# A sort moved from behind a gather pass to behind the first experts, its transposes split over single PSUM banks, and one comparison reading its numbers from PSUM

## The chip, the cores and the metric

One Trainium2 chip, one of its cores. The time is the device time of one execution in microseconds (us), the median of three runs. The engines are named as in the profile: PE is the matrix engine (PEld its weight loads), DVE the vector engine, ACT the scalar engine, POOL the engine that issues the indirect DMAs, SP the queue for most plain DMAs. [...]

## The reference

A graph network of two layers on 6250 nodes with 256 features each, all in float32. Cut to the order of the work:

```python
edge_index = jnp.stack([src, dst])            # 100000 edges, 6250 nodes
xn = layernorm(x)
x = x + hconv2(xn, edges, edge_weight) + mix0(xn)      # layer 0: two convolutions, each
                                                       # h = relu(x @ w1 + b1)
                                                       # agg = segment_sum(ew * h[src], dst)
                                                       # h = relu(bn(agg @ w2 + b2))
x = x + ffn0(layernorm(x))                    # 8 experts, top 2 by a softmax gate
xn = layernorm(x)
x = x + gnn1(xn, edges, edge_attr) + mix1(xn) # gnn1: z_in[in_deg] + z_out[out_deg]
                                              #   + two sigmoid terms
                                              #   + segment_sum(edge_attr @ W_sum + b_sum, src)
x = x + ffn1(layernorm(x), edge_index2)       # 131072 edges of its own: attention over them
                                              # gives the gates of 4 experts
```

The list that this change moves is `edge_index2`, the edge list of the last layer: it has to be sorted by destination before the attention can run over it.

## The kernel before

The nodes lie in 49 tiles of 128. The node features `xa` stay on chip the whole time; `BT` holds a transposed working copy.

**Stages, in order of time.** (1) `first`: layer norm, transposes and the first dense product of every tile; the product goes to a DRAM table. (2) The first edge pass, in `aggregate(1, 0.75)`. (3) `convolve` and the second table. (4) The second edge pass, in `aggregate(2, 0.65)`. (5) `convolve`, then `gating`, which ends with the gates of the first experts. (6) `middle`: the eight first experts, with the edge sums of the second layer beside them. (7) `between` and `gat`: the second mixing, the attention over the sorted list, the four last experts.

**An edge pass** (`edge_pass`) takes 782 groups of 128 edges. For a group, POOL gathers 128 rows into one of 15 ring buffers (L751), DVE writes a 128x128 one-hot matrix by comparing `self.numbers`, which is 0 to 127 in PSUM, with the node of every edge (L591, L593 in `mark`), and PE multiplies rows by one-hot into the PSUM tile `es`, four groups to one tile (L578). DVE adds each finished tile into `BT` (L569). `es` has two banks. In the first pass ACT scales the rows by the edge weights (L615) and one more product counts degrees (L586). A row has 1024 bytes in the first two passes and 512 in the third, which runs in stage (6) and has one product to a group in place of two.

**The order around these passes is written out by hand.** Inside `manual_schedule`, each turn of the edge loop, or each step of the experts, calls `self.step(us)`. This runs the generator that was given to `after_this` until it has issued work worth `us`; what a piece is worth is the number that the piece yields. These numbers are estimates in the code and not measured times. `beside(work, other, rate)` weaves two generators: for every unit that `work` yields, `other` is given `rate` units. At the end `finish()` issues what is left.

In `experts` there are 808 steps: for every expert and every quad of tiles four steps with a first product (L1149, then Gelu on ACT, L1151) and for every tile one step with a second product (L1157) and two additions on DVE (L1161). The one tag `mm` of PSUM tiles serves both products; in stage (6) it has four buffers.

**The sort** (`bitonic`) holds 131072 keys as a 128x1024 tile and runs 153 stages of compare and exchange, each two DVE instructions of 128x512 (L216 and L217), or four of 128x256 (L224), from one tile `sx` to another, `sy`, or back. Where the exchange distance runs over partitions, `across` transposes the tile in eight pieces on PE (L230) into the PSUM tile `back`, which has two banks and one buffer, and ACT copies it back (L232); that happens 14 times in a sort. The kernel sorts twice: `sort_src` behind the first edge pass, after `mix0`, and `sort_gat` (`edge_index2`) behind the second, after `out_degrees`.

`out_degrees` counts how many edges leave each node: one DVE instruction makes eight one-hot matrices (L1175, 98 times), PE sums them over the partitions (L1181), and DVE adds the row to `deg` (L1186).

In stage (6) the generator beside the edge sums is `others()`: `gat_places` finds where each node's run begins in the sorted list (49 small counts, L701, then 49 gathers of 512 KB and counts of 1024 elements, L715), and `node_terms` makes the sigmoid and degree terms of the second layer (L1228 to L1242) and writes them to DRAM (L1243).

[...] `psum(mm, es)` shares them out: up to stage (4) `mm` 2, `es` 2, `kv` 1, `numbers` 1 and `back` 2; in stages (5) and (6) `mm` 4, `es` 2 and `numbers` 1, the stage having no `kv`.

Of the kernel before, what the change touches and what calls it, by code (L numbers as in the profile page):

```python
# [8 lines left out]
F32 = mybir.dt.float32  # L9
# [8 lines left out]
P = 128  # L18
# [33 lines left out]
class Net:  # L52
# [17 lines left out]

    def tr(self):
        return self.mm()

    def back(self):
        return self.ps.tile([P, 2, 512], F32, tag="back", name="back", bufs=1)

    def bcast(self, src, n):

# [123 lines left out]
    def bitonic(self, x, y, out):  # L202
# [4 lines left out]
        nc = self.nc  # L207
        cur, nxt = x, y
# [16 lines left out]
                                                   op0=OP.mult, op1=op)  # L225

        def across(src, dst):
            ps = self.back()
            for j in range(8):
                nc.tensor.transpose(ps[:, j // 4, j % 4 * P:(j % 4 + 1) * P], src[:, j * P:(j + 1) * P], self.ident)  # L230
            for i in range(2):
                nc.scalar.copy(dst[:, i * 512:(i + 1) * 512], ps[:, i, :])  # L232

        a, b = halves(cur, 2)
        nc.vector.tensor_scalar(b, b, -1.0, None, op0=OP.mult)
        yield 0.6
        for k in range(1, 18):
            if k > 10:
                across(cur, nxt)
                cur, nxt = nxt, cur  # L240
                yield 4.0
                for q in range(k - 11, -1, -1):
                    src = cur
                    if q < k - 11:
                        plain(src, nxt, 1 << q)
                    elif k < 17:
                        turned(src, nxt, 1 << q)
                    else:
# [5 lines left out]
                across(cur, nxt)  # L254
                cur, nxt = nxt, cur
                yield 4.0
            for d in range(min(k, 10) - 1, -1, -1):
                src = cur
                if k == 1 or k > 10 or d < k - 1:
                    plain(src, nxt, 1 << d)  # L260
                elif k < 10:
                    turned(src, nxt, 1 << d)
                else:

                    (a, b), (lo, hi) = halves(src, 1 << d), halves(nxt, 1 << d)
                    nc.vector.tensor_scalar(a, a, self.turn[:, 0:1], None, op0=OP.mult)
                    nc.vector.scalar_tensor_tensor(lo, b, self.turn[:, 1:2], a, op0=OP.mult, op1=OP.min)
                    nc.vector.scalar_tensor_tensor(hi, b, self.turn[:, 1:2], a, op0=OP.mult, op1=OP.max)
                cur, nxt = nxt, cur
                yield 1.3  # L270
# [259 lines left out]
    def sort_gat(self, pool):  # L530


        nc = self.nc
# [4 lines left out]
        xi, yi = x.bitcast(I32), y.bitcast(I32)  # L538
        nc.sync.dma_start(xi, ei[1].rearrange("(p w) -> p w", p=P))
        nc.sync.dma_start(yi, ei[0].rearrange("(p w) -> p w", p=P))  # L540
        yield 1.0
        nc.vector.tensor_scalar(xi, xi, NP - 1, None, op0=OP.min)
        nc.vector.tensor_scalar(xi, xi, NODE_BITS, NODE_ONE, op0=OP.logical_shift_left, op1=OP.bitwise_or)
        yield 2.0
# [137 lines left out]
    def gat_places(self, sp):  # L682
# [8 lines left out]
        nc.vector.tensor_scalar(li, li, NODE_BITS, NODE_ONE, op0=OP.logical_shift_left, op1=OP.bitwise_or)  # L691
        heads = sp.tile([P, 1], F32, name="heads")
        nc.sync.dma_start(heads.bitcast(I32), self.by_gat[:, 0:1])
        ph = self.tr()
        nc.tensor.transpose(ph[:, 0:P], heads.to_broadcast([P, P]), self.ident)
        hrow = sp.tile([P, P], F32, name="hrow")
        nc.vector.tensor_copy(hrow, ph[:, 0:P])  # L697
        runs = sp.tile([P, NT], F32, name="gruns")
# [187 lines left out]
    def aggregate(self, layer, us):  # L886
# [3 lines left out]
        with self.tc.tile_pool(name="degree", bufs=1) as dp:  # L890
# [4 lines left out]
            with self.tc.tile_pool(name="edges", bufs=1) as ep, self.tc.tile_pool(name="behind", bufs=1) as bp:  # L895
                if layer == 1:
                    self.after_this(self.mix0(bp), self.sort_src(bp))
                else:
                    self.after_this(self.out_degrees(bp, deg), self.sort_gat(bp))
                with self.tc.manual_schedule():  # L900
                    for _ in self.edge_pass(ep, self.BT, mine, self.table, self.src_of, self.node_of, self.w_of,
                                            self.base1, us):
# [266 lines left out]
    def out_degrees(self, pool, deg):  # L1169

        nc = self.nc
        for k0 in range(0, W1C, 8):
            n = min(8, W1C - k0)
            hot = pool.tile([P, 8, P], BF16, name="ohot", bufs=2)
            nc.vector.tensor_tensor(hot[:, 0:n, :], self.iota.unsqueeze(1).to_broadcast([P, n, P]),  # L1175
                                    self.from_of[:, k0:k0 + n].unsqueeze(2).to_broadcast([P, n, P]), op=OP.is_equal)
            yield 1.1
            ps = self.mm()
# [68 lines left out]
    def middle(self, scales, sums):  # L1247
# [4 lines left out]
        with self.tc.tile_pool(name="experts", bufs=1) as ep:  # L1252
# [2 lines left out]
            self.norms1 = self.norms(sums, "mix1")  # L1255
            with self.tc.tile_pool(name="edge", bufs=1, reuse_waits="tile") as edge:
                def others():
                    yield from self.alone(self.gat_places)
                    yield from self.alone(self.node_terms)
                self.after_this(self.beside(self.edge_sums(edge), others(), 0.45))  # L1260
                with self.tc.tile_pool(name="ffn0", bufs=1, reuse_waits="tile") as pool:
                    self.experts(pool, self.BT, g, 1.7)
        self.edge_pass_if(self.wide2, self.sumsT, None, self.a["edge_attr_128"], self.by_src,
                          EDGE_BITS, E1 - 1, None)

# [525 lines left out]
    def run(self):  # L1791
# [3 lines left out]
        self.load_x()  # L1795
        with tc.tile_pool(name="keep", bufs=1, side="right") as keep, ExitStack() as until:
            self.BT = keep.tile([P, 2, NP], F32, name="BT")
            with self.psum(2, 2) as self.ps:
                self.count_up()
                lists = until.enter_context(tc.tile_pool(name="lists", bufs=1, side="right"))  # L1800
                self.edge_of = lists.tile([P, NG * GE], I32, name="edge_of")
# [45 lines left out]
```

## Time and profile before

| | us |
|---|---|
| median of three runs | 6544.78 (6537.61 to 6550.44) |
| the profiled execution, its own time | 6529.97 |
| its span, first to last instruction | 6528.2 |
| second edge pass, first to last gather | 1607.9 to 2790.8 |
| first experts with the third edge pass | 2959 to 4544 |
| busy: PE, PEld, DVE, ACT, POOL | 4489.9, 3254.1, 3020.2, 1195.9, 3459.5 |

The profile is of one execution. A group of instructions is named by line, engine and operation, with output and inputs; behind it stand the busy time, the mean duration in ns and the idle time of the engine just before, with what ended it. The windows view gives the busy time of each engine in a stretch of time, with the number of instructions in brackets, the clock granted to PE (1 is full speed) and the share of time that the DMA engines were busy. "remote" and "another core or an unknown queue" name a releaser that the profile doesn't identify. A product in float32 shows as two PE instructions.

### The profile page before, as it was taken

The numbers are of one execution on the slowest core, as the hardware profiler recorded it, in microseconds if no ns is written. First come the engines' busy times: TensorE is split into PE (matmuls) and PEld (weight loads), VectorE is DVE, ScalarE is ACT, GpSimd is POOL, SyncE is SP. The second block draws the span as 40 slices with busy tenths as digits, with TensorE's granted clock in tenths as the row PEclk, the third lists the DMA queues.
The fourth block names the chain that finished last, engine by engine and source line by source line (L and its number), as shares of the span: only waits on it lengthen the run. The fifth ranks groups of instructions, "written<-read, shape, count | busy, mean of one in ns | idle before, by whom it ended". The sixth has DMA issues, their size and how long they took to land. (4 is left out here: it accounts for less than half of the span.)

```text
span 6528.2 us, 60427 instructions
## 1 busy us (share of the span) xinstructions
PE 4489.9 (69%) x19240; PEld 3254.1 (50%) x19240; DVE 3020.2 (46%) x8077; ACT 1195.9 (18%) x2327; POOL 3459.5 (53%) x3404
## 2 busy tenths in 40 slices
PE   3788687786656555479989999999932654555560
PEld 2566565554554445456667677676810332333340
DVE  5666465526676556265544555556500111111136
ACT  1333233334000000052111222212300111111120
POOL 0566477751777777604546556564257345554402
PEclk9767756668886766668999999999965777777685
DMA  4433322231332233321341222211221111111134
GB/s 152 126 102 100 99 85 85 86 93 52 89 87 84 85 88 90 91 65 54 118 85 50 63 65 65 64 49 47 71 57 16 38 33 34 33 40 33 34 106 148
DMA packets 356303, 483.23 MB, mean 74 GB/s; under 512 B 114311, under 2 KB 268598, under 8 KB 355926
## 3 DMA queue, kind: packets, MB, share of 16 engines
q0 software_dynamic: 140688, 305.56, 17.7%
q1 hardware_dynamic: 181308, 150.91, 7.8%
q10 hardware_dynamic: 33948, 22.47, 1.1%
q8 instruction: 164, 2.69, 0.2%
q14 instruction: 195, 1.60, 0.1%
HBM read 393.78 MB, written 85.31 MB: 73 GB/s over the span
## 5 line engine op out<-in xcount | busy, mean ns | idle before, releaser
L751 POOL DMA_INDIRECT ring<-table,src_of x1564 | 1701.4, 1088 | 1086.9 <-issue 313.2
L578 PE MATMUL es<-hot,ring 128*128 128x128 f32 x7820 | 1702.8, 352 | 542.6 <-DVE BT L569 192.0
L578 PEld LDWEIGHTS es<-hot,ring 128*128 128x128 f32 x7820 | 1393.7, 242 | 884.0 <-issue 406.3
L751 POOL DMA_INDIRECT G<-gtab,glist x800 | 766.0, 957 | 678.2 <-DVE msg L1572 401.7
L751 POOL DMA_INDIRECT ring<-in_edge_attr,edge_of x782 | 747.2, 955 | 686.5 <-PE es L578 291.5
L1764 PE MATMUL mm<-lw,lhT 128*128 128x256 f32 x1568 | 441.8, 411 | 611.0 <-ACT lhT L1758 336.1
L1157 PE MATMUL mm<-mw,hT 128*128 128x256 f32 x3136 | 747.5, 381 | 23.8 <-DVE xa L1161 20.4
L1149 PE MATMUL mm<-BT,mw 128*128 128x512 f32 (+1 forms) x1664 | 748.6, 573 | 10.0 <-DVE hrow L697 6.3
L1764 PEld LDWEIGHTS mm<-lw,lhT 128*128 128x128 f32 x1568 | 318.2, 205 | 795.5 <-issue 406.0
L1766 DVE TENSOR_TENSOR ly<-mm,lb 128x256 f32<-128x256 f32 x196 | 81.0, 422 | 1324.4 <-remote 553.3
L1157 PEld LDWEIGHTS mm<-mw,hT 128*128 128x128 f32 x3136 | 573.4, 192 | 115.8 <-DVE xa L1161 23.5
L1756 PE MATMUL mm<-lxt,lw 128*128 128x512 f32 (+1 forms) x832 | 425.1, 628 | 118.3 <-issue 116.2
L1151 ACT ACTIVATE hT<-mm,mb 128x512 f32<-128x512 f32 (+1 forms) x416 | 273.0, 661 | 1078.8 <-PE mm L1149 664.9
L1161 DVE SCALAR_TENSOR_TENSOR xa<-mm,gates,xa 128x256 f32<-128x256 f32 x392 | 189.1, 482 | 589.5 <-PE mm L1157 280.7
L615 ACT ACTIVATE ring<-ring,w_of 128x256 f32<-128x256 f32 x782 | 368.2, 502 | 491.1 <-DMA ring<-table,src_of 432.3
L569 DVE TENSOR_TENSOR BT<-BT,es 128x256 f32 x392 | 162.4, 414 | 501.1 <-remote 259.2
L1149 PEld LDWEIGHTS mm<-BT,mw 128*128 128x128 f32 x1664 | 287.0, 193 | 202.9 <-issue 188.2
L1758 ACT ACTIVATE lhT<-mm,lb 128x512 f32<-128x512 f32 (+1 forms) x208 | 135.9, 663 | 1315.9 <-remote 655.7
L593 DVE TENSOR_SCALAR hot<-numbers,node_of,w_of 128x128 f32<-128x128 f32 x782 | 291.2, 402 | 142.2 <-remote 67.3
L591 DVE TENSOR_SCALAR hot<-numbers,node_of 128x128 f32<-128x128 f32 x782 | 247.3, 338 | 165.7 <-PE es L578 101.9
L1756 PEld LDWEIGHTS mm<-lxt,lw 128*128 128x128 f32 x832 | 169.7, 210 | 254.1 <-issue 241.0
L591 DVE TENSOR_SCALAR hot<-numbers,from_of 128x128 f32<-128x128 f32 x782 | 249.9, 343 | 0.0
(854 smaller groups left out, 4315.9 us busy)
## 6 DMA issues: line engine op xcount, KB each, us to landing
ring<-table,src_of POOLq DMA_INDIRECT x1564
ye<-ly SPq DMA_DIRECT2D x48, 512.0 KB
yes<-ye SPq DMA_DIRECT2D x48, 512.0 KB
G<-gtab,glist POOLq DMA_INDIRECT x800
table<-h SPq DMA_DIRECT2D x98, 128.0 KB
ring<-in_edge_attr,edge_of POOLq DMA_INDIRECT x782
grows<-gs SPq DMA_DIRECT2D x10, 960.0 KB
mw<-in_L_ffn_W SPq DMA_DIRECT2D x16, 512.0 KB
```

The lines of the kernel that those rows point to most:

```text
L569: nc.vector.tensor_tensor(dst, dst, ps[:, 0:h * P].rearrange("p (j n) -> p j n", j=h), op=OP.add)
L578: nc.tensor.matmul(ps[:, j * P:(j + 1) * P], lhsT=rows[:, j * P:(j + 1) * P], rhs=hot, start=(first and j == 0), stop=(last and j == h - 1))
L591: self.nc.vector.tensor_scalar(dst, self.numbers, node, None, op0=OP.is_equal)
L593: self.nc.vector.tensor_scalar(dst, self.numbers, node, w, op0=OP.is_equal, op1=OP.mult)
L615: nc.scalar.activation(r, r, AF.Copy, scale=w[:, i:i + 1])
L751: self.nc.gpsimd.indirect_dma_start(out=dst, out_offset=None, in_=table, in_offset=bass.IndirectOffsetOnAxis(ap=idx, axis=0))
L1149: nc.tensor.matmul(ph[:, :n * P], lhsT=w1[:, j, c * P:(c + 1) * P], rhs=xT[:, j, t * P:(t + n) * P], start=(j == 0), stop=(j == 1))
L1151: nc.scalar.activation(hT[:, c, :n * P], ph[:, :n * P], AF.Gelu, bias=b1[:, e, c:c + 1])
L1157: nc.tensor.matmul(po[:, :C], lhsT=h0[:, i, c * P:(c + 1) * P], rhs=w0[:, i, :], start=(i == 0), stop=(i == 3))
L1161: nc.vector.scalar_tensor_tensor(x, y, g[:, t0 + c, e0:e0 + 1], x, op0=OP.mult, op1=OP.add)
L1756: nc.tensor.matmul(ph[:, :n * P], lhsT=w1[:, e, j, c * P:(c + 1) * P], rhs=xt[:, j, :n * P], start=(j == 0), stop=(j == 1))
L1764: nc.tensor.matmul(po[:, :C], lhsT=h0[:, i, c * P:(c + 1) * P], rhs=w2[:, e0, i, :], start=(i == 0), stop=(i == 3))
```

## The change

`sort_gat` is no longer given to the second edge pass. It becomes the first part of `others()` in stage (6), in its own pool, ahead of `gat_places`. The rates of that stage are set anew: `beside` gets 0.85 in place of 0.45, and a step of the experts is worth 2.2 in place of 1.7.

`across` no longer has a tile of two banks of its own. It takes two ordinary `mm` tiles of one bank each, and it yields in three places (4.0, 2.0, 2.0) where it was issued in one piece and its caller yielded 4.0 after it. Both sorts use it. The two banks set free go to `mm`: four in place of two up to the end of stage (4). In stages (5) and (6) `mm` gets five in place of four.

`out_degrees` compares with `self.numbers` in PSUM where it compared with `self.iota` in SBUF. `gat_places` yields 12.0 between loading the heads of the list and transposing them, and 3.0 before copying the transpose out.

```diff
         def across(src, dst):
-            ps = self.back()
+            yield 4.0
+            ps = [self.mm(), self.mm()]
             for j in range(8):
-                nc.tensor.transpose(ps[:, j // 4, j % 4 * P:(j % 4 + 1) * P], src[:, j * P:(j + 1) * P], self.ident)
+                nc.tensor.transpose(ps[j // 4][:, j % 4 * P:(j % 4 + 1) * P], src[:, j * P:(j + 1) * P], self.ident)
+            yield 2.0
             for i in range(2):
-                nc.scalar.copy(dst[:, i * 512:(i + 1) * 512], ps[:, i, :])
+                nc.scalar.copy(dst[:, i * 512:(i + 1) * 512], ps[i])
+            yield 2.0
...
-                across(cur, nxt)
+                yield from across(cur, nxt)
                 cur, nxt = nxt, cur
-                yield 4.0
...
         nc.sync.dma_start(xi, ei[1].rearrange("(p w) -> p w", p=P))
         nc.sync.dma_start(yi, ei[0].rearrange("(p w) -> p w", p=P))
-        yield 1.0
+        yield 10.0
...
         nc.sync.dma_start(heads.bitcast(I32), self.by_gat[:, 0:1])
+        yield 12.0
         ph = self.tr()
         nc.tensor.transpose(ph[:, 0:P], heads.to_broadcast([P, P]), self.ident)
+        yield 3.0
...
-                    self.after_this(self.out_degrees(bp, deg), self.sort_gat(bp))
+                    self.after_this(self.out_degrees(bp, deg))
...
-            nc.vector.tensor_tensor(hot[:, 0:n, :], self.iota.unsqueeze(1).to_broadcast([P, n, P]),
+            nc.vector.tensor_tensor(hot[:, 0:n, :], self.numbers.unsqueeze(1).to_broadcast([P, n, P]),
...
                 def others():
+                    yield from self.alone(self.sort_gat)
                     yield from self.alone(self.gat_places)
                     yield from self.alone(self.node_terms)
-                self.after_this(self.beside(self.edge_sums(edge), others(), 0.45))
+                self.after_this(self.beside(self.edge_sums(edge), others(), 0.85))
...
-                    self.experts(pool, self.BT, g, 1.7)
+                    self.experts(pool, self.BT, g, 2.2)
...
-            with self.psum(2, 2) as self.ps:
+            with self.psum(4, 2) as self.ps:
...
-                with self.psum(4, 2) as self.ps:
+                with self.psum(5, 2) as self.ps:
```

More of the change, by code (lines that the diff above doesn't have):

```diff
@@ L72, in tr @@
         return self.mm()
-    def back(self):
-        return self.ps.tile([P, 2, 512], F32, tag="back", name="back", bufs=1)
     def bcast(self, src, n):
@@ L253, in bitonic @@
                     yield 1.3
-                across(cur, nxt)
+                yield from across(cur, nxt)
                 cur, nxt = nxt, cur
-                yield 4.0
             for d in range(min(k, 10) - 1, -1, -1):
```

## The prediction, made before the changed kernel ran

> **What bounds the kernel now.** The change touches two stages, so I read the windows view by stage first. The second edge pass is cut where its companion work changes: beside `out_degrees` (1606 to 1984), beside the sort (1984 to 2598), alone (2598 to 2790). The first table holds the ring's instructions alone, the POOL column being the gathers.
>
> ```profile
> 1606.00:1984.00 378.00, 166.81 (x996) 143.80 (x996) 0.00 (x0) 290.55 (x251) 0.85 0.31 88
> 1984.00:2598.00 614.00, 326.84 (x1592) 280.04 (x1592) 0.00 (x0) 451.73 (x397) 0.68 0.30 85
> 2598.00:2790.00 192.00, 96.62 (x515) 87.69 (x514) 0.00 (x0) 126.40 (x134) 0.68 0.32 94
> ```
>
> Per gather that is 378/251 = 1.506 us, 614/397 = 1.547 us and 192/134 = 1.433 us; POOL is busy for 1.157, 1.138 and 0.943 us of each. So a gather is 0.2 us longer beside the companions, yet the pass alone is only 0.11 us a gather faster: something else stops it. The timeline shows both, first beside the sort, then alone.
>
> ```profile
> 2069.57 0.68 DVE L216 TENSOR_TENSOR sy<-sx 128x512 f32<-128x512 f32 x1
> 2070.17 0.69 DVE L217 TENSOR_TENSOR sy<-sx 128x512 f32<-128x512 f32 x1
> 2070.25 1.43 POOL L751 DMA_INDIRECT ring<-table,src_of  x1 [0.30 <-issue]
> 2070.77 0.73 DVE L593 TENSOR_SCALAR hot<-numbers,node_of,w_of 128x128 f32<-128x128 f32 x2
> ...
> 2710.54 0.95 POOL L751 DMA_INDIRECT ring<-table,src_of  x1 [0.30 <-issue]
> 2713.68 0.42 DVE L569 TENSOR_TENSOR BT<-BT,es 128x256 f32 x1 [13.63 <-remote]
> 2714.16 3.78 PE L578 MATMUL es<-hot,ring 128*128 128x128 f32 x16 [10.19 <-issue]
> 2718.19 0.94 POOL L751 DMA_INDIRECT ring<-table,src_of  x1 [3.33 <-PE es L578]
> ```
>
> A gather that meets the sort's two SBUF operands takes 1.43 us and more; alone it takes 0.95 with 0.30 to the next, a floor of 1.25. Then DVE stands 13.63 us for an unnamed releaser, PE with it, the ring fills and POOL waits 3.33 us.
>
> The first experts, in the table with all engines:
>
> ```profile
> 3510.00:4310.00 800.00, 796.46 (x3296) 559.85 (x3295) 459.06 (x1244) 175.81 (x316) 471.51 (x488) 1.00 0.22 63
> 4310.00:4522.00 212.00, 211.28 (x923) 151.41 (x922) 118.21 (x366) 36.15 (x56) 135.88 (x143) 1.00 0.17 45
> ```
>
> PE is busy for 99.6% at full clock. This stage is bound by PE, and all added to PE is paid in full. A step there, from the timeline:
>
> ```profile
> 3906.16 1.88 PE L1149 MATMUL mm<-BT,mw 128*128 128x512 f32 x4
> 3907.88 0.38 PE L578 MATMUL es<-hot,ring 128*128 128x128 f32 x2
> 3908.10 1.89 PE L1157 MATMUL mm<-mw,hT 128*128 128x256 f32 x8
> ```
>
> From start to start a step is 1.72 us and an edge group 0.22. 808 x 1.72 + 782 x 0.22 = 1562 us; the stage took 1585 (2959 to 4544). The rest is two waits: 6.3 us for `hrow` at the start, 20.1 us where DVE waits 30.1 us for `gend` in `gat_places`.
>
> [...] 1.43 us beside L216/L217, 0.95 beside L569 (SBUF and PSUM) and L593. [...] The page counts 164 and 195 packets on two instruction queues, and stalls of 10 to 14 us recur on PE and DVE; that these are fetches isn't shown.
>
> **The change, part by part.** I sum against the profiled execution, 6529.97 us, which is 15 us under the median of 6544.78; the same difference is then taken from the median.
>
> *Second pass, sort gone.* Removed: 153 compare stages on DVE, 112 transposes, 28 ACT copies, three DMAs on SP. 397 gathers go from 1.547 to the 1.433 of the stretch alone: **-45 us**. Bounds: the unaccompanied end of the first pass (1308 to 1446, 94 gathers) ran at 1.468, giving -31; the floor of 1.25 gives -118. I take 1.433, as the stalls stay.
>
> *Second pass, numbers in PSUM.* L1175 (98 x 1.203 us) now has one SBUF input, so it should no longer hold up gathers: 251 x (1.157 - 0.943) = 54 us of POOL. But beside it PE has 7.1 instructions a gather (1770/251) against 3.8, and DVE is busy for 265 of 378 us, so other stalls take over. I take 1.47 in place of 1.506: **-9 us**. Bounds: 1.433 gives -18[...].
>
> *First pass, `across` in three pieces.* Before, ACT stood behind transposes just issued: at 954 it had waited 14.8 us and then ran 12 row scalings in one burst. `sort_src` becomes 14 x 4 = 56 units longer: (259.7 of `mix0` + 316.5)/0.75 = 768 turns of 793, so it still ends inside the pass. The pass beside the sort runs at 493/318 = 1.55 us a gather, POOL's own 375.9/318 + 0.30 = 1.48; at most 22 us are there. **-10 us** (0 to -22).
>
> *Two more `mm` banks in stages 1 to 4.* PE waited for DVE to free a bank 15.6 us at L851 and 10.4 us at L158, mostly hidden. **-4 us** (0 to -12).
>
> *First experts, PE.* 14 x 8 = 112 transposes; sixteen took 3.41 us at full clock (4553.81), 0.21 each: **+24 us**, no cover. The `hrow` wait goes, since 12 units now lie between load and transpose: **-6 us**. The `gend` wait stays.
>
> *First experts, pacing.* Units: `sort_gat` 325.5, `gat_places` 122.3, `node_terms` 254.5, together 702; edges 793 x 1.27 = 1007. 1709 of 808 x 2.2 = 1778, so all ends by step 777, and nothing is left for `finish`. While both run, a step carries 2.2/1.85 = 1.19 units of edges (0.94 groups; before 1.7/1.45 = 1.17) and 1.01 of others (before 0.53). After step 695 a step carries 1.73 groups, PE needs 2.1 us and POOL 1.73 x 1.25 = 2.16; **+3 us** (0 to 8).
>
> *First experts, DVE.* Without others DVE's share is (459 - 154 us of `node_terms` groups)/412 steps = 0.74 us a step. A compare stage takes 1.20 us from start to start (1.43 for L224) and 1.01/1.3 = 0.78 of one falls to a step: 0.95. 1.69 of 1.93 us, 88%. In `gat_places` 1.35 us per 1.68 steps make 80%. In `node_terms` 3.14 us per 4.5 steps make 75%; before L1228 DVE waited 42 us in 49 tiles for the `terms` write, with half the distance now maybe 2 us each, which makes 98%. Behind DVE's waits stand the additions L1161, which free `mm`; five banks are five steps, some 9 us of slack. So short lags are hidden, lasting ones not: **+15 us** (0 to +60).
>
> *Queues.* SP gets two loads and a store of 512 KB each; behind them stand the next expert's weights, wanted over 100 us later, and the ten units (some 19 us) cover the loads. POOL has only the longer gathers: at 1.8 us against 1.93 x 1.06 = 2.05 a group it holds. Where `gat_places` reuses the sort's memory, its iota and the DVE instruction after it wait for the list's store, about 5 us, within the slack: **+2 us** (0 to 5).
>
> Sum: -45 - 9 - 10 - 4 + 24 - 6 + 3 + 15 + 2 = **-30 us**: 6500 for a profiled execution, **6515** as a median.
>
> **Rivals.**
> 1. *The second pass keeps its pace.* Stalls, not gathers, set it, and the sort's stretch comes only to 1.49 (-23), `out_degrees` and the first pass give nothing: -23 - 4 + 38 = +11, about 6556. For it: a 0.2 us longer gather showed as only 0.11. Against: the stretch alone is in the trace. Its lesser form is that the PSUM operand frees nothing, 9 us.
> 2. *DVE becomes the bound of the first experts* (slower). It decides from 1.93 us a step, 0.24 more than I count. Counted by durations (0.68 each) the compare stages come to 0.74 + 1.06 = 1.80, and L224 and PE waits may bring 2.1: 322 steps x 0.17 = 55, and `node_terms` 252 x 0.07 = 18. +73 in place of +15 makes +28, about 6573. [...] Against: five banks.
> 3. *POOL's floor is reached*: 1.35 and 1.30 us a gather give -137 in place of -54, about 6432. Against: stalls in the stretch alone.
>
> **From cases to numbers.** Main case 0.60, rival 1 0.15, rival 2 0.19, rival 3 0.06. 0.2% is 13 us, about what a measurement can tell from no change. The main case's own range is 6475 to 6545, a little of it inside 13 us. Faster 0.64, same 0.15, slower 0.21. The range 6465 to 6575 leaves out most of rival 3 and the upper half of rival 2.
>
> **What would show it.** Second pass: 782 gathers in about 1130 us (now 1183), gathers beside `out_degrees` at 0.95. First experts: about 38 us longer, 112 transposes of 0.21 us, no `hrow` wait, DVE near 85% in its first 600 us and PE still over 97%. I am wrong if the second pass falls by under 30 us, or if PE there idles long before L1149 or L1157 on DVE.

## The result, and the profile after

The changed kernel takes **6653.89 us** (median of four runs, 6649.62 to 6658.03) where the kernel before takes 6541.19 on the same chip: a ratio of **1.0171, 95% interval 1.0153 to 1.0189**. It is 113 us slower. I had forecast 30 us faster. The profiled execution of it has a span of 6656.2 us and took 6658.03.

Two things have to be told apart, and the runs below do that. The experts' new pacing filled POOL's queue; and on the chip of this result PE, ACT and DVE stand while POOL's queue is nearly full (PE busy for 84 to 88% of the time). On a second kind of chip, met later, they don't (99.8% with edges alone), and there the same changed kernel is 94 us *faster* than before.

First the second edge pass, the ring's instructions alone, POOL fifth, as in the first table of the prediction; beside `out_degrees`, then alone, since the sort is gone. Line numbers are shifted by two: L576 is the edge product that was L578, L567 was L569, L589 was L591, and L228 is the transpose of `across`.

```profile
1616.00:2015.00 399.00, 176.32 (x992) 155.60 (x992) 0.00 (x0) 246.37 (x260) 0.80 0.30 86
2015.00:2773.00 758.00, 369.06 (x2096) 350.15 (x2096) 0.00 (x0) 494.19 (x522) 0.71 0.31 91
```

POOL is now busy for 246.37/260 = 0.948 us of a gather beside `out_degrees` (1.157 before), and yet a gather there takes 399/260 = 1.535 us (1.506 before). The rest runs at 758/522 = 1.452 us, near the 1.433 of the stretch alone before. First to last gather the pass went from 1183 to 1155 us.

Then the first experts, all engines (PE, PEld, DVE, ACT, POOL): beside the sort, beside `gat_places`, beside `node_terms`, and with edges alone.

```profile
3000.00:3600.00 600.00, 600.00 (x2553) 425.85 (x2553) 410.95 (x1011) 119.62 (x188) 289.82 (x295) 1.00 0.15 40
3600.00:3850.00 250.00, 209.06 (x797) 142.85 (x795) 141.35 (x370) 34.64 (x54) 134.30 (x141) 0.91 0.50 132
3850.00:4360.00 510.00, 450.62 (x1750) 306.47 (x1751) 292.50 (x797) 103.18 (x202) 290.61 (x298) 0.94 0.26 67
4360.00:4610.00 250.00, 219.57 (x912) 154.07 (x911) 131.66 (x401) 37.48 (x63) 158.00 (x164) 0.95 0.19 50
```

Beside the sort PE is busy for 600 of 600 us at full clock: the sort in its new place costs nothing but its transposes. From its end on PE is busy for 84 to 88% where it was 97 to 99% before, and the clock falls under 1. The stage took 1585 us before (2959 to 4544) and takes 1740 now (2929 to 4669). All that lies ahead of it gained 30 us. The whole stage, before and then after:

```profile
2959.00:4544.00 1585.00, 1544.96 (x6386) 1087.31 (x6385) 869.89 (x2432) 310.99 (x520) 887.78 (x927) 0.98 0.25 66
2929.00:4669.00 1740.00, 1608.84 (x6500) 1118.67 (x6500) 1057.69 (x2776) 323.26 (x548) 906.34 (x928) 0.96 0.23 61
```

PE's idle time rises from 40 to 131 us, and its busy time by 64 us, of which the sort's transposes are 14.5; its mean clock falls from 0.98 to 0.96.

What stops PE there is seen in the timeline of all engines but PEld, in the last of these stretches, where only edge gathers are left beside the experts:

```profile
4494.98 1.89 PE L1157 MATMUL mm<-mw,hT 128*128 128x256 f32 x8
...
4496.93 1.88 PE L1149 MATMUL mm<-BT,mw 128*128 128x512 f32 x4
...
4499.09 1.89 PE L1157 MATMUL mm<-mw,hT 128*128 128x256 f32 x8
...
4501.21 0.95 POOL L751 DMA_INDIRECT ring<-in_edge_attr,edge_of  x1 [0.30 <-issue]
...
4502.99 0.38 PE L576 MATMUL es<-hot,ring 128*128 128x128 f32 x2
4504.29 0.48 DVE L1161 SCALAR_TENSOR_TENSOR xa<-mm,gates,xa 128x256 f32<-128x256 f32 x1 [8.58 <-PE es L576]
4504.39 0.69 ACT L1151 ACTIVATE hT<-mm,mb 128x512 f32<-128x512 f32 x1 [6.46 <-PE es L576]
4504.57 0.95 POOL L751 DMA_INDIRECT ring<-in_edge_attr,edge_of  x1 [2.41 <-PE es L576]
...
4508.65 0.29 DVE L567 TENSOR_TENSOR sumsT<-sumsT,es 128x128 f32 x1
...
4509.03 0.77 PE L576 MATMUL es<-hot,ring 128*128 128x128 f32 x2 [5.66 <-issue]
```

The product L1157 of 4494.98 ends at 4496.87, and PE goes on to the next ones. The addition on DVE that waits for it starts at 4504.29, 7.4 us later. The Gelu waits for the product L1149 that ended at 4498.81 and starts 5.6 us later. DVE, ACT and POOL are released within 0.3 us of each other, 2.1 to 2.4 us after POOL's last gather of a run had ended (4502.16). Meanwhile PE has used up its buffers and stands until 4509.03. What it lacks is a bank of `es`: DVE adds the finished tile (L567) only at 4508.65, behind the late additions, and PE goes on 0.1 us after that ended. The profile's "issue" hides this: from 3600 to 4640 PE stood for over 0.3 us before L576 31 times, 51.6 us in all, and 24 of these stalls (47.2 us) ended within 0.1 us of an L567.

The program has one engine wait for another by semaphores, and the trace also holds the times at which their updates were recorded. PE ended twelve instructions that update its semaphore between 4495 and 4504.2; updates were recorded at 4497.16, 4498.58 and 4499.99, and then seven from 4504.27 to 4504.59. So by the record PE's signal itself is late, and not the engines that heed it: DVE starts at 4504.29. Nor is it a single case: in the median a Gelu started 2.9 us after its product from 3600 to 4610 (220 Gelus), and 0.04 us after it beside the sort. For 41% of PE's signalling instructions from 3600 to 4640 no update was recorded within 1 us, beside the sort for 4%. These shares are rough, since some updates are missing from the record (832 for 970 instructions).

The time after such a stall is lost in part too. Windows view of the same place; the column after the five engines is the clock granted to PE:

```profile
4497.00:4502.00 5.00, 5.00 (x23) 3.49 (x23) 0.00 (x0) 0.69 (x1) 3.78 (x5) 1.00 0.20 52
4504.00:4508.00 4.00, 0.00 (x0) 0.00 (x0) 3.53 (x10) 1.37 (x2) 2.82 (x3) 1.00 0.12 33
4509.00:4515.00 6.00, 5.97 (x14) 4.39 (x15) 2.35 (x8) 0.00 (x0) 4.19 (x5) 0.50 0.18 44
4516.00:4520.00 4.00, 4.00 (x21) 3.03 (x20) 1.55 (x5) 0.69 (x1) 2.69 (x3) 1.00 0.12 34
```

After 5.66 us without work (4503.37 to 4509.03) PE runs its next 6 us at a clock of 0.50, which loses 3 us more: eight instructions of L1157 take 3.62 us from 4509.59 on, and 1.89 at 4499.09. Full clock came back some 6 us after PE went on (1.00 from 4516 on).

### The profile page after: what moved, and what is told of

Same layout as the page of the kernel before. It is cut to its first block, busy times and chain, and to the rows that moved or that the text cites. A ratio compares the mean times of both kernels' runs of the same rounds, so it can differ in the third digit from the quotient of the medians.

```text
span 6656.2 us, 60585 instructions
## 1 busy us (share of the span) xinstructions
PE 4453.6 (67%) x19240; PEld 3236.4 (49%) x19240; DVE 3019.9 (45%) x8077; ACT 1193.7 (18%) x2327; POOL 3350.9 (50%) x3404
## 5 line engine op out<-in xcount | busy, mean ns | idle before, releaser
L751 POOL DMA_INDIRECT ring<-table,src_of x1564 | 1573.7, 1006 | 1197.5 <-issue 328.9
L576 PE MATMUL es<-hot,ring 128*128 128x128 f32 x7820 | 1644.7, 349 | 635.6 <-DVE BT L567 247.5
L576 PEld LDWEIGHTS es<-hot,ring 128*128 128x128 f32 x7820 | 1376.6, 244 | 939.4 <-issue 489.8
L751 POOL DMA_INDIRECT ring<-in_edge_attr,edge_of x782 | 765.0, 978 | 738.2 <-PE es L576 384.9
L1157 PE MATMUL mm<-mw,hT 128*128 128x256 f32 x3136 | 768.9, 388 | 65.4 <-DVE xa L1161 24.1
L1149 PE MATMUL mm<-BT,mw 128*128 128x512 f32 (+1 forms) x1664 | 765.3, 582 | 13.0 <-issue 10.3
L1157 PEld LDWEIGHTS mm<-mw,hT 128*128 128x128 f32 x3136 | 583.7, 195 | 176.9 <-issue 57.6
L1161 DVE SCALAR_TENSOR_TENSOR xa<-mm,gates,xa 128x256 f32<-128x256 f32 x392 | 188.5, 481 | 530.4 <-PE mm L1157 294.0
L567 DVE TENSOR_TENSOR BT<-BT,es 128x256 f32 x392 | 162.3, 414 | 578.6 <-remote 380.0
L1149 PEld LDWEIGHTS mm<-BT,mw 128*128 128x128 f32 x1664 | 293.5, 196 | 214.4 <-issue 206.6
L591 DVE TENSOR_SCALAR hot<-numbers,node_of,w_of 128x128 f32<-128x128 f32 x782 | 288.4, 401 | 213.6 <-PE es L576 124.7
L589 DVE TENSOR_SCALAR hot<-numbers,node_of 128x128 f32<-128x128 f32 x782 | 246.6, 338 | 165.9 <-PE es L576 73.0
L589 DVE TENSOR_SCALAR hot<-numbers,from_of 128x128 f32<-128x128 f32 x782 | 251.7, 343 | 1.6 <-PE es L576 1.6
```

The source lines that it names most:

```text
L567: nc.vector.tensor_tensor(dst, dst, ps[:, 0:h * P].rearrange("p (j n) -> p j n", j=h), op=OP.add)
L576: nc.tensor.matmul(ps[:, j * P:(j + 1) * P], lhsT=rows[:, j * P:(j + 1) * P], rhs=hot, start=(first and j == 0), stop=(last and j == h - 1))
L589: self.nc.vector.tensor_scalar(dst, self.numbers, node, None, op0=OP.is_equal)
L591: self.nc.vector.tensor_scalar(dst, self.numbers, node, w, op0=OP.is_equal, op1=OP.mult)
L751: self.nc.gpsimd.indirect_dma_start(out=dst, out_offset=None, in_=table, in_offset=bass.IndirectOffsetOnAxis(ap=idx, axis=0))
L1149: nc.tensor.matmul(ph[:, :n * P], lhsT=w1[:, j, c * P:(c + 1) * P], rhs=xT[:, j, t * P:(t + n) * P], start=(j == 0), stop=(j == 1))
```

## The experiments

**The theories.** The runs met two kinds of chip, called first and second kind here: the chip of the result and two others are of the first, two more of the second. S: a run of gathers without a pause on POOL holds back the signals by which PE tells ACT, DVE and POOL that a product is done. L: POOL is only too slow and PE waits for rows. T: the bytes of the gathers do it. C: DVE and ACT have twice the companion work in a step, and PE waits for them. Last, the sort itself.

### The pacing alone, without the sort (b_before_dense)

```diff
-self.after_this(self.beside(self.edge_sums(edge), others(), 0.45))
+self.after_this(self.beside(self.edge_sums(edge), others(), 0.85))
-    self.experts(pool, self.BT, g, 1.7)
+    self.experts(pool, self.BT, g, 2.2)
```

> The kernel before with nothing of the change but its two numbers of pacing, 0.85 and 2.2; the sort stays behind the second pass. Theory S: 623 of 808 steps carry 1.4 to 1.7 gathers each, POOL has no pause in them, and at 0.3 to 0.5 us a step (as the changed kernel shows) the stage is 150 to 230 us longer, 6690 to 6770 in all. Rival C: the companions are as dense for 373 steps, then gone: 100 to 150 us longer, and no stalls in the part with edges alone. If instead the sort in that place is the cause, the time stays within 20 us of the kernel before.

6758.42 us, 1.0333 (1.0316 to 1.0350) of before: 226 us slower, at the upper end of what S gave. The stage took 1822 us. Stretches beside `gat_places`, beside `node_terms`, and with edges alone:

```profile
3000.00:3250.00 250.00, 199.61 (x769) 137.55 (x767) 140.59 (x374) 33.71 (x52) 130.90 (x138) 0.90 0.49 132
3350.00:3750.00 400.00, 354.38 (x1381) 243.29 (x1379) 241.95 (x648) 84.93 (x170) 240.01 (x244) 0.95 0.25 72
3850.00:4400.00 550.00, 479.30 (x2033) 339.28 (x2032) 216.49 (x678) 72.93 (x110) 358.83 (x377) 0.94 0.19 50
```

PE falls to 80, 89 and 87%. In the last stretch there is no companion at all and DVE is busy for 39%: the two numbers of pacing do the harm, neither the sort nor C.

### The big gathers taken off POOL (a_sp_rows)

```diff
-                self.gather(r.bitcast(I32), self.by_gat, run[:, t:t + 1])
+                self.nc.sync.dma_start(r.bitcast(I32), self.by_gat)
...
-                    self.gather(z[i], a[name], idx[:, i, t:t + 1])
+                    self.nc.sync.dma_start(z[i], a[name][0:P, :])
```

Two iotas on POOL, not shown, put the fixed numbers in place.

> The changed kernel, but the 49 grow rows (512 KB each) and the 98 zg rows of the first experts come by plain transfers of the same size on SP, so POOL has only the edge gathers there; the rows are not the addressed ones and the places of the nodes are replaced by fixed numbers, so the counts and terms are not those of the reference. Theory S (a run of gathers without a pause on POOL holds back the signals of PE; DVE, ACT and PE then stand until POOL pauses): beside gat_places and node_terms POOL has 0.94 x 1.25 = 1.18 us of gathers in a step of 1.9 us and pauses at nearly every one, so PE is back over 97% there and the kernel 100 to 120 us faster than the changed one, 6535 to 6555; the part where edges run alone at 1.73 groups a step keeps its stalls. Rival T (the bytes of the big gathers hold things up) and rival C (DVE and ACT get twice the companion work a step and PE waits for them): bytes and companion work are the same, so within 20 us of 6654.

6525.24 us, 0.9997 (0.9987 to 1.0008) of before: the loss is gone, and the time is 10 us below the range that S gave. Beside the `grow` rows, beside the `zg` rows, and with edges alone:

```profile
3620.00:3770.00 150.00, 150.00 (x627) 105.74 (x626) 118.11 (x268) 27.57 (x42) 68.92 (x73) 1.00 0.64 202
3880.00:4290.00 410.00, 404.90 (x1687) 285.20 (x1687) 298.32 (x800) 104.72 (x205) 198.42 (x204) 1.00 0.29 84
4300.00:4450.00 150.00, 129.18 (x533) 90.94 (x532) 71.41 (x228) 20.87 (x31) 96.75 (x103) 0.95 0.17 46
```

In the first line PE is busy for every microsecond while 202 GB/s move (last column) and DVE does the same companion work as in the changed kernel, for 79% of the time. In the third, where nothing was taken off POOL, PE is at 86% with 46 GB/s. So neither T nor C holds; what counts is how much POOL issues. Whether that is the time for which it issues, or the transfers of its own queue that are then under way, no run separates: both go with a gather.

### Rows of 4 bytes (h_tiny, h_tiny_b)

```diff
+        if h == 1:
+            for r in ring:
+                nc.vector.memset(r, 0.0)
...
+                if h == 1:
+                    self.gather(ring[k % RING][:, 0:1], self.a["edge_weight"].rearrange("(e o) -> e o", o=1), idx[:, k:k + 1])
+                else:
```

> The changed kernel, but each edge row of the third pass is one number of 4 bytes in place of 128, gathered by the same list into the same buffers (the rest of a row is zero, so the edge sums are not the reference's). The number of gathers, their descriptors and every wait stay; 399 of 402 KB of each eight groups' traffic, and so nearly all of the pass's bytes, go. Theory S: the stalls stay, 6630 to 6660. Rival T (bytes): the part with edges alone, where nothing else moves, loses its stalls, and the others some: 6560 to 6610.

(Eight groups move 512 KB in 128-element rows and 4 KB here; the figures in that text are wrong.) h_tiny ran on a chip of the second kind; h_tiny_b is the same kernel on the first.

> The changed kernel with edge rows of 4 bytes in the third pass (the edge sums are not the reference's), beside the changed kernel on one chip. On a chip of the first kind: theory S says the stalls stay, within 25 us of the changed kernel; rival T says 50 to 100 us faster. On the second kind there is nothing to lose: within 10 us.

h_tiny_b, first kind: 6657.34 us, 1.0182 (1.0164 to 1.0200), the changed kernel beside it 6649.12. Edges alone:

```profile
4410.00:4600.00 190.00, 161.01 (x685) 116.07 (x685) 92.53 (x294) 25.16 (x39) 121.55 (x129) 0.94 0.02 2
```

2 GB/s, and PE still at 85%; POOL issues 129 gathers in 190 us, as densely as in the changed kernel (164 in 250). T falls for good. h_tiny, second kind: 5666.25 us, ratio 0.9826 (0.9808 to 0.9844), no different from the changed kernel there.

### The length of the ring (d_ring8, f_ring23, f_ring23_b)

```diff
-        ring = [pool.tile([P, h * P], F32, name=f"ring{i}") for i in range(RING)]
+        size = RING if h == 2 else RING3          # RING3 = 8; in f_ring23: RING2 = 23 if h == 2, else RING
+        ring = [pool.tile([P, h * P], F32, name=f"ring{i}") for i in range(size)]
...
-        far = RING - 4
+        far = size - 4
```

> The changed kernel with 8 ring buffers in place of 15 in the third edge pass alone (gathers run at most 8 groups ahead of the product that frees a buffer; the one-hots keep their lead of 8). Theory S: a run of gathers without a pause is at most 4 to 6 long in place of 8 to 13, PE's buffered work covers it, and most of the stalls go: 6550 to 6590. Rival L (POOL is simply too slow and PE waits for rows): less run-ahead can only make the waits longer, 6655 to 6720. Rivals T and C: no change, within 20 us of 6654.

6642.70 us, 1.0170 (1.0153 to 1.0187): no change. My number for S was wrong, and by itself this run is what T and C had; it is the runs above that speak against those. With edges alone POOL's long runs were still 7 to 11 gathers with eight buffers, as with 15: some signals do come through in between (three in the case above), so a run isn't bounded by the ring.

> The changed kernel with 23 ring buffers in place of 15 in the first two edge passes. Alone, the second pass runs in bursts of 13 gathers without a pause, then POOL waits about 2 us, in all 17.5 us for 12 to 13 gathers. If the pause is one for each ring (theory S as it stands), bursts become 21 long and a gather 0.06 us shorter on 1564 gathers: 6545 to 6625. If the run is not limited by the ring but by how fast the signals come (as 8 buffers in the third pass would say, which changed nothing), no change, 6640 to 6665.

> The changed kernel with 23 ring buffers in the first two passes, beside it on one chip. First kind: 30 to 110 us faster if a pause comes once a ring, no change if the run is not set by the ring. Second kind: within 10 us, as POOL runs near its floor of 1.25 us a gather there already.

f_ring23_b, first kind: 6659.64 us, 1.0176 (1.0157 to 1.0195); f_ring23, second kind: 5665.61, 0.9828 (0.9809 to 0.9847). No change on either; on the first kind the second pass still runs in bursts of mostly 13, as with 15 buffers. So S holds in the form "late while POOL is kept issuing", not as "one pause for each ring". That a pause of POOL lets the signals through is not shown: pause and signals come together, and in the pauses POOL itself waits for PE or an unnamed releaser. L is right in one respect: with its pauses, POOL comes to 1.4 to 1.5 us a gather and no better, with 8, 15 or 23 buffers.

### The two kinds of chip (after_again, after_c)

> The changed kernel itself, beside the kernel before on one chip, because the last four kernels met a chip on which the kernel before takes 5763 us in place of 6541 and stands for an unnamed releaser almost nowhere. If this is a chip of the first kind (before near 6540), the ratio is 1.015 to 1.019 as on record. On one of the second kind PE's signals are not late, the prediction's sum holds and more: 80 to 110 us faster than before, a ratio near 0.983.

> The changed kernel once more, as the reference of this set. First kind of chip (before near 6540): ratio 1.015 to 1.019. Second kind (before near 5763): 0.981 to 0.985, since the stalls that eat the gain are not there.

after_again: 6649.12 us, 1.0166 (1.0146 to 1.0186), before 6542.42. after_c: 5666.55 us, **0.9836 (0.9819 to 0.9852)**, before 5760.18. The same program, and the sign turns. Edges alone on the second kind, after a stretch beside the sort, then the timeline of PE's first products, DVE, ACT and POOL in it:

```profile
2700.00:3250.00 550.00, 550.00 (x2348) 391.04 (x2347) 373.71 (x892) 111.32 (x176) 260.21 (x267) 1.00 0.15 40
...
4000.00:4140.00 140.00, 139.77 (x616) 99.25 (x616) 84.62 (x268) 23.36 (x34) 105.86 (x113) 1.00 0.21 53
```

```profile
4061.49 1.88 PE L1149 MATMUL mm<-BT,mw 128*128 128x512 f32 x4
...
4063.00 0.94 POOL L751 DMA_INDIRECT ring<-in_edge_attr,edge_of  x1 [0.30 <-DMA ring<-in_edge_attr,edge_of]
...
4063.41 0.69 ACT L1151 ACTIVATE hT<-mm,mb 128x512 f32<-128x512 f32 x1 [3.37 <-PE mm L1149]
...
4064.25 0.95 POOL L751 DMA_INDIRECT ring<-in_edge_attr,edge_of  x1 [0.31 <-issue]
```

POOL issues 113 gathers in 140 us, 1.24 us each, with no pause, and PE is busy for 99.8%. The Gelu starts 0.04 us after its product ended (4063.37); on the first kind it was 5.6. The recorded updates of PE's semaphore differ in the same way: on the second kind each came within 0.24 us of an instruction's end (3250 to 4190, 0.01 us in the median), on the first they are late themselves (none within 1 us for 41% of the instructions). The median Gelu, from 3290 to 4140, starts 0.04 us after its product there, against 2.9 on the first kind. Which step before the recorded update is late, and why on one kind of chip only, no run shows.

### The same work, paced by gathers (c_balanced, g_cover, g_cover_b)

```diff
 def others():
+    self.rate = 0.37
-    yield from self.alone(self.sort_gat)
+    yield from self.scaled(self.alone(self.sort_gat), 0.5)       # g_cover: 0.45
+    self.rate = 1.1
-    yield from self.alone(self.gat_places)
+    yield from self.scaled(self.alone(self.gat_places), 1.12)    # 1.35
+    self.rate = 0.71                                             # 0.65
-    yield from self.alone(self.node_terms)
+    yield from self.scaled(self.alone(self.node_terms), 1.2)     # 1.1
...
-    self.experts(pool, self.BT, g, 2.2)
+    self.experts(pool, self.BT, g, 2.0)
```

`beside` takes its rate from `self.rate`, and `scaled` multiplies what a piece yields. g_cover also yields 15.0 between the load of `gend` and its first use.

> The changed kernel with its first experts paced by the gathers: a step carries 1.15 edge groups beside the sort, 0.75 beside gat_places and 0.92 beside node_terms, so POOL has 1.4 to 1.5 us of gathers a step everywhere and the edges end with the companions; the same instructions otherwise. Theory S: PE over 98% busy from the end of the sort on, the stage about 1610 us in place of 1740, 6525 to 6560 in all. Rival C: the companion work a step falls only from 1.01 to 0.94 and 0.69 units, so about half of the loss stays, 6590 to 6620. Rival T: bytes a second are lower by a third beside the terms only, 6600 to 6640.

6551.45 us, 1.0027 (1.0017 to 1.0037): about 100 us of the loss is back, as S had it. PE, though, stays at 94% beside `gat_places` and 96% beside `node_terms`, not over the 98% that I gave. Its profiled execution took 6530.42, 21 us under its own median, so its stage time of 1629 us flatters it.

> The balanced kernel with three changes of its pacing: 15 units of other work between the load of gend and its first use (PE stood 21 us there, DVE 29), the sort a tenth quicker, the grow gathers a fifth further apart. Theory S: the 21 us go and most of some 15 us of stalls beside the grow gathers, so 20 to 40 us under the balanced kernel, 6505 to 6535. If the stalls beside the grow gathers come of their bytes instead, only the 21 us and what the lower density spares: 6525 to 6540.

> The balanced kernel with the cover for gend, beside the changed kernel. First kind: 120 to 150 us faster than the changed one, 0.995 to 1.000 of the kernel before. Second kind: about 20 us faster than the changed one, the wait for gend alone.

g_cover_b, first kind: **6530.09 us, 0.9984 (0.9972 to 0.9996)**. g_cover, second kind: **5646.62, 0.9794 (0.9774 to 0.9813)**. It is under both kernels on both kinds; on the first it is 119 us under the changed kernel (I gave 120 to 150) and less than 0.2% under the kernel before. g_cover_b beside `gat_places` and `node_terms`:

```profile
3500.00:3750.00 250.00, 238.32 (x966) 166.25 (x965) 153.56 (x435) 42.17 (x66) 131.72 (x140) 0.98 0.36 122
3850.00:4450.00 600.00, 571.38 (x2339) 398.06 (x2338) 351.52 (x974) 126.21 (x234) 361.97 (x373) 0.99 0.21 63
```

PE is at 95%. Set against POOL's booking, which is gathers a step by the units x 1.25 us over the step's products on PE (1.93 us, 2.1 with edges alone), the first kind gives a curve, falling though not smooth (before: 294.9 of 304 us from 3046 to 3350 and 902.9 of 910 from 3400 to 4310):

| kernel and stretch | POOL booked | PE busy |
|---|---|---|
| a_sp_rows, `grow` rows | 0.61 | 100% |
| before, `node_terms` | 0.75 | 99% |
| g_cover_b, `gat_places` | 0.78 | 95% |
| c_balanced, `node_terms` | 0.79 | 96% |
| before, `gat_places` | 0.80 | 97% |
| g_cover_b, `node_terms` | 0.82 | 95% |
| c_balanced, `gat_places` | 0.84 | 94% |
| after, `node_terms` | 0.90 | 88% |
| after, `gat_places` | 0.99 | 84% |
| after, edges alone | 1.03 | 88% |

### The operand in PSUM (e_iota, e_iota_b, e_iota_c)

```diff
-            nc.vector.tensor_tensor(hot[:, 0:n, :], self.numbers.unsqueeze(1).to_broadcast([P, n, P]),
+            nc.vector.tensor_tensor(hot[:, 0:n, :], self.iota.unsqueeze(1).to_broadcast([P, n, P]),
```

> The changed kernel with the one-hots of out_degrees compared with the iota in SBUF again. The gathers beside it become 0.2 us longer (1.157 in place of 0.947 us of POOL each). By the prediction's step this costs 9 us or more, up to 50 if the freed POOL time counted: 6663 to 6705. By theory S the time POOL got back there is only spent in pauses behind PE (the stretch took 1.54 us a gather in place of 1.51), so the operand is worth nothing: 6640 to 6660.

> The changed kernel with the iota in SBUF for out_degrees again. First kind: the POOL time that the PSUM operand sets free is spent in pauses, so within 12 us of the changed kernel either way. Second kind: 45 to 65 us slower than the changed kernel (the prediction's step gave it 9).

> The changed kernel with the iota in SBUF again. First kind: within 12 us of the changed kernel's 1.0166 to 1.0171, so 1.015 to 1.019, since the time that POOL gets back goes into pauses. If it counted as on the second kind, 50 us slower: 1.024 to 1.026. Second kind: 0.991 to 0.995 again.

All three met the second kind: 5731.41, 5718.90 and 5716.17 us, ratios 0.9941 (0.9923 to 0.9959), 0.9926 (0.9910 to 0.9943) and 0.9911 (0.9885 to 0.9937). Beside after_c on one chip the SBUF operand costs 5718.90 - 5666.55 = **52 us**. The ring's instructions beside `out_degrees`, e_iota_b and then after_c:

```profile
1480.00:1780.00 300.00, 158.55 (x812) 123.31 (x812) 0.00 (x0) 238.16 (x204) 0.87 0.31 90
```

```profile
1480.00:1780.00 300.00, 164.86 (x959) 129.23 (x960) 0.00 (x0) 226.89 (x241) 0.95 0.37 106
```

204 gathers against 241 in the same 300 us: 1.47 and 1.245 us each. For the first kind I have only traces: from its first to its last L1175 `out_degrees` lasts 489 and 508 us with the iota (before, b_before_dense) and 512 and 512 with PSUM (after, after_again). Six more traces of this kind with PSUM have 509 to 517. It gives nothing there, by these traces; it wasn't tried by itself.

### Every edit but the move (j_old_place, j_old_place_b, k_old_place_cover)

```diff
-                    self.after_this(self.out_degrees(bp, deg))
+                    self.after_this(self.out_degrees(bp, deg), self.sort_gat(bp))
...
-                    yield from self.alone(self.sort_gat)
...
-                self.after_this(self.beside(self.edge_sums(edge), others(), 0.85))
+                self.after_this(self.beside(self.edge_sums(edge), others(), 0.45))
...
-                    self.experts(pool, self.BT, g, 2.2)
+                    self.experts(pool, self.BT, g, 1.7)
```

> Every edit of the change but the move: the sort stays behind the second pass, pacing 0.45 and 1.7, numbers in PSUM, across in three pieces, more mm banks. First kind: without the move nothing saturates POOL anew, so within 20 us of the kernel before (6525 to 6555); if the other edits cost something by themselves, above that. Second kind: the PSUM operand's 50 us, 0.988 to 0.994 of before.

> Every edit but the move of the sort, old pacing. First kind of chip: within 20 us of the kernel before (6525 to 6555), so that the loss of the changed kernel is all in the move and its pacing. If the other edits are part of the loss: above 6555. Second kind: 0.985 to 0.989 again.

> The same with 15 units of other work between the load of gend and its use (a step worth 1.74). First kind: 15 to 22 us under j_old_place, so 6505 to 6535; if it is not slower than the balanced kernel with the same cover (6530), moving the sort is worth nothing there. Second kind: 20 us under j_old_place.

These too met the second kind: 5684.76 and 5682.19 us, 0.9869 (0.9852 to 0.9885) and 0.9854 (0.9827 to 0.9881), the first a little under the 0.988 to 0.994 that I gave; k_old_place_cover 5663.53, 0.9832 (0.9816 to 0.9849), 21 us under j_old_place as forecast. On one chip, the move and its pacing take 5684.76 to 5666.55, **-18 us**. The second pass goes from 1015 to 976 us, and the first experts from 1552 to 1585. So the cover for `gend`, with the sort in its old place, gives as much here as the move does. What the edits without the move do on the first kind stays open; that moving the sort pays there at all is not shown, since g_cover_b is only 12 us under the kernel before and holds the cover for a wait of 21 us.

## Why the prediction was wrong, point by point

**Second pass, sort gone (-45).** The stretch went to 1.452 us a gather, not 1.433: 397 x (1.547 - 1.452) = -38 on the chip of the result. On the second kind the whole pass lost 39. Right, a little too large.

**Numbers in PSUM (-9).** On the chip of the result nothing: POOL's 0.21 us a gather came back as pauses, for the reason I gave ("other stalls take over"). On the second kind -52: there the 54 us of POOL's own time counted almost in full, and I had set that aside. What the operand does to POOL shows on both kinds: with `self.numbers` in place of the iota a gather beside `out_degrees` takes 0.948 us of POOL in place of 1.157 on the first, and 226.89/241 = 0.941 in place of 238.16/204 = 1.167 on the second. Gather by gather, in the traces of before and after: those that ran while an L1175 ran took 1.28 us in the mean with the iota and 0.95 with PSUM, those that met none 0.95 in both; those that met a compare of the sort, before, took 1.34 in the mean. What the edit is worth is decided by what stands behind POOL.

**`across` in pieces (-10), more `mm` banks (-4).** Not seen on the first kind: the first pass ended 4 us later than before (1451.5 against 1447.4). On the second, j_old_place is 75 us under the kernel before, which leaves about -23 for both, the `hrow` wait and the fifth bank together (75 - 52).

**Transposes (+24), `hrow` (-6).** The 112 transposes take 14.5 us of PE's own time in the trace after, 0.13 each, not 0.21. I had misread the sixteen that I took the price from: their stretch (4553.6 to 4557.2 in the trace of before) ran at a granted clock of 0.50, not at full clock. The `hrow` wait is gone, the one for `gend` stayed (21.3 us). On the second kind, where PE's longest waits in the stage are 25.1 us for DVE's L1161, once, and 6.5 us for ACT, the stage grew by 33 us for the move; I had said 38.

**DVE (+15, rival 2 up to +73).** Nothing. Beside the sort DVE is busy for 68%, not 88, and PE for 100. Rival 2 forecast a slower kernel, but named the wrong engine: it was on the right side by luck.

**Pacing (+3) and queues ("it holds"): this is the step that failed.** The prediction took POOL for an engine that costs nothing as long as its gathers fit into the step, and put what they do to PE's signals at nothing. I priced POOL in two places and both times with edges alone: 1.73 x 1.25 = 2.16 us where only edges are left, and 1.8 us against 2.05 a group for the sort's part. Between them I never added the others' gathers. Beside `gat_places` 1.01 units a step are 1.01/1.7 = 0.59 `grow` gathers: 0.94 + 0.59 = 1.53, x 1.25 = 1.92 us of a step of 1.93. And I took 1.25, the floor, though the profile of before showed in every stretch of the second pass that a POOL without slack runs at 1.43 or more, with PE and DVE standing meanwhile.

The 13.63 us that I showed there for an unnamed releaser were already this: POOL had issued 16 gathers without a pause from 2693.03 to 2712.74, PE had ended its last product at 2703.97, and of the seven updates of its semaphore due from 2695.8 on the trace has three, at 2699.61, 2706.66 and 2713.66; DVE went on at 2713.68. I left such stalls standing ("as the stalls stay") and did not ask what makes them. At 1.43 the last part alone would have been 1.73 x 1.43 = 2.47 us a step; measured 2.43 (4.72 us from Gelu to Gelu, 808/416 steps each).

But 1.43 would have found only about half of the stage's 155 us. By an estimate from the prediction's steps it gives 121 x (1.53 x 1.43 - 1.93) = 31 us beside `gat_places`, 252 x (1.38 x 1.43 - 1.93) = 11 beside `node_terms` (1.38 is 0.94 and two `zg` gathers in 4.5 steps) and 82 x (2.47 - 2.10) = 30 with edges alone, for in the first two a gather came to 250/141 = 1.77 and 510/298 = 1.71 us: there POOL waits in its turn for PE and DVE. Counted by Gelus in the traces, the stretches lost 42 x (4.77 - 3.93) = 35 us beside the `grow` gathers and 114 x (4.39 - 3.67) = 82 beside `node_terms`, against their spacing before, and 53 x (4.72 - 4.08) = 34 with edges alone, against PE's own work: 151 in all, a rough sum, and the stage is 155 longer.

**What would show it.** I had written that I was wrong if the second pass fell by under 30 us, which it did (28), or if PE idled before L1149 and L1157 on DVE; the largest entry is L576, for 45 us put down to "issue", and there, too, it stood for DVE, as the timeline above shows. DVE had time to spare, though (57% busy beside `gat_places`): it waited for PE's signals. The price of the stage was the deciding term; the pass alone would have left a gain.

On the second kind of chip, where PE is busy for 99.8% with POOL at 1.24 us a gather, the kernel came out 94 us faster than before, near rival 3 ("POOL's floor is reached", 6432, which is 113 under the median before), with gathers at 1.245 and 650/521 = 1.248 us in the second pass. That is rival 3's path, but on a chip that the forecast was not made for.

## What to carry to other kernels

Book the issuing queue like any engine: add up every gather that a step carries, of all generators woven into it, and price one at what a saturated stretch of the trace shows (here 1.43 in an edge pass alone), not at the shortest gap (1.25). Then ask what the other engines do while that queue is full, for by the estimate above that cost about as much again here. When work is moved into a stage and its pacing is raised to fit, everything that comes after it is made denser as well; set the rate for each part by the resource that it uses. A gain that rests on freeing a queue can be worth nothing where the engines behind that queue are what stops it (the operand in PSUM: nothing on the first kind by the traces, 52 us on the second), so look for that first. And repeat a verdict of a few per cent on another chip before you trust its sign (1.017 and 0.984 here).

## What the runs showed of the hardware that I had not expected

- The same program takes 12% less on one kind of chip than on the other (before: 5760 to 5764 us and 6532 to 6545), and the sign of this change differs with it (0.984 and 1.017).
- On the slower kind, while POOL issues indirect DMAs back to back (0.95 us and 0.30 to the next), products on PE are seen by ACT, DVE and POOL late, by 2.9 us in the median of the Gelus from 3600 to 4610 and by 7.4 us in the case shown, many of them in batches, there about 2 us after POOL's last gather. PE's semaphore updates are themselves recorded late (none within 1 us for 41% of the instructions, beside the sort for 4%). The bytes moved don't matter (PE busy for 85% with 2 GB/s, for 86% with 46), nor do SP's transfers of 202 GB/s (PE at 100%). With 0.61 of POOL's time booked PE is at 100%, from 0.75 to 0.84 at 94 to 99, from 0.90 on at 84 to 88; the cause underneath is open.
- A stall of PE of 5.66 us cost about half as much again, in the one case shown: the 6 us after it ran at a clock of 0.50.
